# Moving weight preparation and eight up products of a feed-forward network into the start of a two-layer transformer kernel

## The chip, the cores and the metric

The kernel runs on one core of a Trainium2 chip. The core has five engines that work side by side, each on its own queue of instructions: TensorE (PE, matrix products and transposes; PEld are its weight loads), VectorE (DVE), ScalarE (ACT, activation functions), GpSimd (POOL) and SyncE (SP, which here only issues DMA transfers). The metric is device time in microseconds for one launch. The time before is 1350.04 us, the median of three runs (1349.27 to 1352.81).

## The reference

The input is 2 batches of 1024 tokens with 256 features, float32. Two layers are computed; in each, attention and a feed-forward network (FFN) read the same normalized input, and both are added to it:

```python
xn = _layernorm(x, axis=-1)
x = x + _L0_attn_ref(xn, Wq, Wk, Wv, Wp, bp) + _L0_ffn_ref(xn, W_fc, W_proj)
xn = _layernorm(x, axis=-1)
x = x + _L1_attn_ref(xn, ...) + _L1_ffn_ref(xn, w1, w2, w3)
```

What matters here is layer 0. Its attention has 16 heads of 16 features and is causal. Its FFN first turns its weights into ternary ones, in groups of 64, and then has an up product to 1024 hidden features, a squared relu, an RMS norm, and a down product:

```python
scale = clip(mean(abs(wg)), 1e-08, None)          # wg: groups of 64, in bfloat16
q = clip(round(wg / scale), -1.0, 1.0)
w1 = w + ((q * scale) - w)                        # so for W_fc and for W_proj
h = square(relu(einsum('bsd,hd->bsh', x, w1)))
hn = h * rsqrt(mean(square(h)) + eps)
out = einsum('bsh,dh->bsd', hn, w2)
```

Layer 1 has a latent attention, which makes up the second half of the kernel's time, and an FFN with a sigmoid gate (`sigmoid(x1) * x2`) whose weights are ternary too, with one scale for a whole matrix.

## The kernel before

All work is in float32 and the order on every engine is written out by hand: under `tc.manual_schedule()` each engine executes its instructions in the order in which the Python code emits them. An instruction waits on its own engine until its inputs are there and its output buffer is free, and everything behind it on that engine waits too.

**Tiles.** The tokens lie in 16 tiles of 128 (0 to 7 are batch 0). The rows of `x` are loaded in four transfers, even and odd tiles of each batch (`even`, `odd`, `even1`, `odd1`). `ln_stats` (VectorE statistics, then a square root on ScalarE, L157 to L161), `ln_rstd` (reciprocal on VectorE, L169), `ln_norm` (the normalized pair of tiles, on VectorE or GpSimd, L179, one buffer) and `ln_turn` (transpose on TensorE, L190; copied out by ScalarE, L196) make the transposed input `xnT`.

**Attention.** The heads of one batch are worked on in four groups of four, eight groups in all. For a group, `project` makes keys (1), queries (0) or values (2) on TensorE (L240), evacuates them on ScalarE or VectorE (L248, L250) and writes them to DRAM; `fetch` (L262) reads them back in another order into the buffers `stage`, of which keys and values share one; `permute` (L269 to L273) puts them in their last layout as `head`. Of a batch's four groups, the first two need the even tiles alone, the other two the odd ones. Then come the maxima of the scores for each query (`maxima`, TensorE L313, reduced by VectorE, L324 and L329), `finish` (the maxima are added to the queries as one more row, L338 and L339), and later `scores` (L354), their exponential on ScalarE (L361), a causal mask on GpSimd (L364), and `product` with the values (L379).

The main loop runs over g from -1 to 8 and, within a group, over twelve steps n. In a step of a group, TensorE makes a piece of the maxima of the next group (g + 1), a piece of this group's scores, and a product from two steps back. Round g = -1 has only the maxima of group 0, and the dictionary `first` says what else is done in its steps: projections of the groups 1 to 3, norms, permutes.

**Fill.** `fill` is a list of pieces, one of which is popped in each step of a group: twelve projections of the groups 4 to 7, then for each of four blocks of 512 tokens the FFN of layer 0 as eight `up` products (L436; relu, square and again square on ScalarE, L443 to L449, and an accumulation of squares on GpSimd, L446 and L450) and eight `down` products (L467). From group 6, step 3, on, the FFN of layer 1 for two blocks is added behind (`ffn1`: `up` L578 with a sigmoid on ScalarE, L585; `down` L593). Group 7 has no next group and pops two pieces in each step. What is left is done among the output projections of batch 1.

**Ternary weights.** `ternary(w)` gives four pieces for one half of a weight matrix row block: `begin` (absolute value and sign on ScalarE, L205 and L207), `scale` (a sum over groups on TensorE, L211, then two operations on VectorE), `choose` (VectorE), and `put` (one operation on VectorE, two on GpSimd, L226 to L228). There are eight such steps, `weight_steps`: four for the up weights `wfc`, then four for the down weights `wpr`. `deal` puts a list of pieces into half steps of the main loop, and `slot` runs what is due. Before, all eight were dealt from group 0, step 0, on, one in two steps:

```python
for k, pieces in enumerate(weight_steps):
    deal(0, 2 * k, 0, pieces)
```

Buffers that matter: two pairs of PSUM banks for scores and the maxima of group 0 (`ps_s`), three single banks for all else (`ps_m`), six temporary tiles (`temp`) for evacuated projections, junk outputs, relu and squares, one buffer each for `q_ab`, `q_sg`, `q_sc` and `xn`.

Of the kernel before, what the change touches and what calls it, by code (L numbers as in the profile page):

```python
# [46 lines left out]
def two_layers(ctx: ExitStack, tc: tile.TileContext, a: dict, out: bass.AP):  # L47
    nc = tc.nc
# [57 lines left out]
    with ExitStack() as scope:  # L106
# [4 lines left out]
        NG = 4 * B  # L111
# [39 lines left out]
        xnT = [main.tile([P, KC, S], F32, tag=f"xnT{b}", name=f"xnT0_{b}") for b in range(B)]  # L151
# [11 lines left out]
        def ln_stats(at):  # L163
            for n in range(*at.indices(NT)):
                ln_stat(n)
            ln_root(at)

        def ln_rstd(at):
            nc.vector.reciprocal(rstd[:, at], rstd[:, at])  # L169
# [4 lines left out]
        def ln_norm(n, step=1, engine=nc.vector):  # L174

            xn = l0t.tile([P, SC], F32, tag="xn", name="xn", bufs=1)
            for k in range(2):
                t = n + k * step
                engine.tensor_scalar(  # L179
                    xn[:, k * E : (k + 1) * E], x_sb[:, t, :], mv[:, t, 0:1], rstd[:, t : t + 1],  # L180
                    ALU.subtract, ALU.mult,
                )
            return xn

        def ln_turn(xnT, n, xn, step=1):

            pt = ps_bank()
            for k in range(2):
                for kc in range(KC):
                    nc.tensor.transpose(  # L190
                        pt[:, (2 * kc + k) * P : (2 * kc + k + 1) * P],
                        xn[:, k * E + kc * P : k * E + (kc + 1) * P], ident,
                    )
            at = n % TB
            to = xnT[n // TB].rearrange("p c (n t) -> p c n t", t=P)[:, :, at : at + step + 1 : step, :]
            nc.scalar.copy(to, pt.rearrange("p (c n t) -> p c n t", c=KC, n=2))  # L196
# [61 lines left out]
        def fetch(g, i):  # L258

            src = rows[g, i].rearrange("(j d) t -> d j t", d=D0)  # L260
            for c in range(4):
                nc.sync.dma_start(stage[i][32 * c : 32 * c + D0], src[:, :, GC * c : GC * (c + 1)])  # L262
# [473 lines left out]

        with tc.manual_schedule():

            even, odd, even1, odd1 = EVEN_ODD
            ln_stats(even)  # L740
            ln_rstd(even)
            for n in (0, 4):
                ln_turn(xnT, n, ln_norm(n, 2), 2)
            project(0, 1, nc.vector)
            fetch(0, 1)
            project(0, 0)
            fetch(0, 0)
            ln_stats(odd)
            project(0, 2, nc.vector)
            project(1, 1)  # L750
            ln_stats(even1)
            ln_stats(odd1)
            for at in (odd, even1, odd1):
                ln_rstd(at)
            project(1, 0)
            project(1, 2, nc.vector)
            for n in (1, 5):
                ln_turn(xnT, n, ln_norm(n, 2, nc.gpsimd), 2)
            permute(0, 1)
            permute(0, 0)  # L760

            first = {
                0: [lambda: turns.append(ln_norm(8, 2, nc.gpsimd))],
                1: [lambda: fetch(0, 2), lambda: project(2, 1)],
                2: [lambda: ln_turn(xnT, 8, turns.pop(), 2), lambda: project(2, 0),
                    lambda: turns.append(ln_norm(12, 2, nc.gpsimd))],
                3: [lambda: project(2, 2)],
                4: [lambda: permute(0, 2), lambda: fetch(1, 1), lambda: fetch(1, 0),
                    lambda: ln_turn(xnT, 12, turns.pop(), 2)],
                5: [lambda: project(3, 1), lambda: turns.append(ln_norm(9, 2, nc.gpsimd))],  # L770
                6: [lambda: project(3, 0)],
                7: [lambda: permute(1, 1), lambda: ln_turn(xnT, 9, turns.pop(), 2),
                    lambda: turns.append(ln_norm(13, 2, nc.gpsimd))],
                8: [lambda: permute(1, 0)],
                9: [lambda: project(3, 2), lambda: ln_turn(xnT, 13, turns.pop(), 2)],
            }
            turns = []

            slots = {}

            def deal(g, n, part, pieces):
                for k, f in enumerate(pieces):
                    at = 2 * (12 * g + n) + part + k
                    slots.setdefault((at // 24, at % 24 // 2, at % 2), []).append(f)
# [2 lines left out]
                for f in slots.pop((g, n, part), ()):  # L787
                    f()

            for k, pieces in enumerate(weight_steps):  # L790
                deal(0, 2 * k, 0, pieces)
            deal(2, 4, 0, ternary1("w1"))
            deal(3, 4, 0, ternary1("w2"))
# [9 lines left out]
            for g in range(-1, NG + 1):  # L803
                this, nxt = 0 <= g < NG, g + 1 < NG
                for n in range(12 if g < NG else 2):
                    k = 12 * g + n - 2
                    if g == NG - 2 and n == 3:
                        fill += ffn1(0) + ffn1(1)
                    if g == -1:
                        for f in [maxima(0, n, pair) for pair in ((0, 1), (2, 3))]:  # L810
                            f()
                    elif nxt:
                        for part, (a_, b_) in enumerate((((0, 1), (2, 3)), ((2, 3), (0, 1)))):
                            after = [maxima(g + 1, n, a_), scores(g, n, b_)]
                            for f in after:
                                f()
                            if k >= 0 and part == 0:
                                product(k // 12, k % 12)
                            if part == 0:
                                slot(g, n, 0)  # L820
                    else:
                        if this:
                            after = [scores(g, n, pair) for pair in ((2, 3), (0, 1))]
                            for f in after:
                                f()
                            fill.pop(0)()
                        product(k // 12, k % 12)
                        slot(g, n, 0)
                    if k >= 0 and k % 12 in (3, 11):
# [64 lines left out]
            for i in range(TB):  # L894
                f = project_out(B - 1, i)
                if rest is not None:
                    rest()
                rest = f
                if i % 2 == 0 and fill:
                    pump()  # L900
                    pump()
                else:
                    side.pop(0)()
                if i == 4:
                    ln_stats(four(2))
                if i == 5:
                    ln_rstd(four(2))
                    xnT1.append(main.tile([P, KC, S], F32, tag="xnT1", name="xnT1_1"))
                    xn = ln_norm(8)
                if i == 6:  # L910
                    ln_turn(xnT1, 8, xn)
                    xn = ln_norm(10)
                if i == 7:
                    ln_turn(xnT1, 10, xn)
# [1 line left out]
            ln_stats(four(3))  # L916
            ln_rstd(four(3))
            xn = ln_norm(12)
            side.pop(0)()
            pump()  # L920
            ln_turn(xnT1, 12, xn)
            xn = ln_norm(14)
# [406 lines left out]
```

## Time and profile before

| what | value |
|---|---|
| median of three runs | 1350.04 us |
| the profiled execution | 1347.1 us, its span 1345.4 us |
| PE busy | 1277.3 us (95%) |
| DVE busy | 751.9 us (56%) |
| ACT busy | 673.0 us (50%) |
| POOL busy | 480.6 us (36%) |
| granted TensorE clock, mean | 0.976 |
| first piece of the maxima (L313) | 36.47 us from the start |
| first scores of group 0 (L354) | 79.25 us |
| last up product of group 7 (L578) | 588.15 us |

The busy time of an engine is the time in which it had an instruction at work, and at a lower clock the same work is longer busy. TensorE is busy for most of the span; where it isn't, or where its clock is below 1, time can be gained. The page gives the span in 40 slices of 33.6 us.

### The profile page before, as it was taken

How to read it: one execution, taken by the hardware profiler on the slowest of the kernel's cores; microseconds unless marked ns; L12 is line 12 of the kernel's file. 1: busy time of each engine (PE TensorE's matmuls, PEld its weight loads, DVE VectorE, ACT ScalarE, POOL GpSimd, SP SyncE). 2: the span in 40 equal slices, each digit the busy share in tenths (PEclk: the TensorE clock that was granted, in tenths of full speed). 3: DMA queues.
4: the chain of work that ended last, by engine and by line, in shares of the span. 5: the costliest groups of instructions: out<-in, count | busy, mean ns of one | idle time of the engine just before them, and what ended most of it. 6: DMA issues, size and time to landing. Idle time of an engine off the chain costs nothing.

```text
span 1345.4 us, 36539 instructions
## 1 busy us (share of the span) xinstructions
PE 1277.3 (95%) x15722; PEld 794.5 (59%) x15722; DVE 751.9 (56%) x1879; ACT 673.0 (50%) x1250; POOL 480.6 (36%) x506
## 2 busy tenths in 40 slices
PE   5899999999999999999998799999999999999996
PEld 3454445464564643556757467777666767767665
DVE  3557755565465562124335676666656666666572
ACT  1235664646537556554233565555455555555541
POOL 4333733543224221010231444433444434444310
PEclk9779999999999998999998999999999999999998
DMA  7221301011010000001043000000000000000000
GB/s 230 55 56 55 95 1 25 1 25 16 10 16 9 25 1 20 17 1 59 1 145 74 14 18 11 14 22 11 22 15 22 7 26 10 27 10 15 15 6 22
DMA packets 65810, 41.11 MB, mean 31 GB/s; under 512 B 37841, under 2 KB 63185, under 8 KB 65393
## 3 DMA queue, kind: packets, MB, share of 16 engines
q1 hardware_dynamic: 64800, 35.51, 10.5%
q8 instruction: 123, 2.02, 0.6%
q0 software_dynamic: 416, 2.49, 0.5%
q10 hardware_dynamic: 432, 0.79, 0.2%
q14 instruction: 39, 0.31, 0.1%
HBM read 26.18 MB, written 10.49 MB: 27 GB/s over the span
## 4 chain that ended last, share of the span: by engine, by line
PE 82%; DVE 5%; ACT 3%; issue 3%; POOL 1%; DVEq 0%; ACTq 0%; POOLq 0%
PE ps_s L1090 15%; PE ps_m L313 12%; PE ps_o L1138 11%; PE ps_m L578 6%; PE ps_o L379 5%; PE ps_t L1030 5%; PE ps_m L467 5%; PE ps_m L436 5%; PE ps_m L593 3%; PE ps_t L1023 3%; PE ps_t L1165 3%; DVE p L1097 2%; PE ps_m L240 2%; DVE pT L1107 1%; ACT p L1101 1%
## 5 line engine op out<-in xcount | busy, mean ns | idle before, releaser
L1101 ACT ACTIVATE p<-p,nmax 128x1024 f32<-128x1024 f32 (+7 forms) x256 | 197.2, 771 | 210.7 <-DVE nmax L1097 209.8
L1090 PE MATMUL ps_s<-kT,qc 128*128 128x512 f32 (+3 forms) x768 | 280.9, 499 | 19.0 <-DVE nmax L1097 10.3
L1097 DVE CUSTOM_DVE_ANT_0 p<-ps_s,wpe 128x1024 f32<-128x1024 f32 (+7 forms) x256 | 184.9, 745 | 176.5 <-PE ps_s L1090 175.5
L361 ACT ACTIVATE p<-ps_s 128x1024 f32<-128x1024 f32 (+1 forms) x192 | 153.0, 809 | 138.0 <-PE ps_s L354 133.1
L1090 PEld LDWEIGHTS ps_s<-kT,qc 128*128 128x128 f32 x768 | 131.2, 191 | 130.8 <-issue 94.6
L1107 DVE STREAM_TRANSPOSE pT<-p 128x1024 f32<-128x1024 f32 (+7 forms) x256 | 185.9, 758 | 22.1 <-ACT p L1101 21.0
L313 PE MATMUL ps_m<-head,head 16*128 16x512 f32 (+3 forms) x672 | 180.4, 539 | 2.8 <-DVE nmx L324 1.2
L354 PE MATMUL ps_s<-head,head 17*128 17x512 f32 (+3 forms) x768 | 167.0, 539 | 0.0
L1138 PE MATMUL ps_o<-pT,vrep 32*64 32x128 f32 x9216 | 153.5, 276 | 7.3 <-issue 4.5
L1138 PEld LDWEIGHTS ps_o<-pT,vrep 32*64 32x64 f32 x9216 | 136.1, 132 | 35.8 <-issue 28.7
L1063 POOL TENSOR_TENSOR qc<-t,t 32x512 f32<-32x512 f32 x120 | 152.4, 1270 | 8.1
L364 POOL TENSOR_SCALAR_AFFINE_SELECT p<-p 128x256 f32<-128x256 f32 x128 | 55.1, 436 | 219.7 <-ACT p L361 219.3
L1058 POOL TENSOR_TENSOR t<-t,cosq 128x512 f32<-128x512 f32 x28 | 35.7, 1273 | 257.9 <-issue 143.9
L313 PEld LDWEIGHTS ps_m<-head,head 16*128 16x128 f32 x672 | 68.8, 185 | 91.6 <-issue 31.5
L578 PE MATMUL ps_m<-xnT,w 128*128 128x512 f32 x192 | 94.3, 619 | 0.0
L329 DVE TENSOR_REDUCE nmx<-ps_m 128x1 f32<-128x512 f32 x112 | 72.3, 686 | 38.0 <-PE ps_s L354 28.8
L324 DVE CUSTOM_DVE_ANT_0 junk<-ps_m,maskz,nmx 128x512 f32<-128x512 f32 (+3 forms) x112 | 57.7, 548 | 47.3 <-PE ps_s L354 33.0
L379 PE MATMUL ps_o<-p,v 128*32 128x512 f32 (+3 forms) x768 | 82.5, 502 | 0.0
L467 PEld LDWEIGHTS ps_m<-wpr,hT 128*128 128x128 f32 x512 | 59.9, 191 | 16.6 <-DVE nmx L324 6.0
L467 PE MATMUL ps_m<-wpr,hT 128*128 128x128 f32 x512 | 66.6, 282 | 0.0
L1165 PE MATMUL ps_t<-wvo,xT 128*128 128x256 f32 x256 | 62.3, 387 | 4.4 <-DVE nmax L1097 2.6
L324 DVE CUSTOM_DVE_ANT_0 junk<-ps_m,maskz 128x512 f32<-128x512 f32 (+3 forms) x112 | 50.6, 488 | 27.8 <-PE ps_s L354 22.6
(172 smaller groups left out, 1783.2 us busy)
## 6 DMA issues: line engine op xcount, KB each, us to landing
rows<-proj SPq DMA_DIRECT2D x24, 256.0 KB, 2.2
stage<-rows SPq DMA_DIRECT2D x96, 64.0 KB, 3.2
w<-in_w SPq DMA_DIRECT2D x3, 768.0 KB, 5.0
x_sb<-in_x SPq DMA_DIRECT2D x4, 512.0 KB, 12.2
x<-x_sb SPq DMA_DIRECT2D x4, 512.0 KB, 3.2
fold_wo<-in_wo SPq DMA_DIRECT2D x8, 256.0 KB, 3.1
vrep<-kv SPq DMA_DIRECT2D x32, 64.0 KB, 2.1
xin<-x SPq DMA_DIRECT2D x16, 128.0 KB, 2.2
```

The source lines that it names most:

```text
L313: nc.tensor.matmul(t[:, :w], quad(q, c, D0)[:, i * P : (i + 1) * P], quad(k, c, D0)[:, k0 : k0 + w], start=True, stop=True, tile_position= ...
L354: nc.tensor.matmul(t[:, c % 2, :w], quad(k, c, D0 + 1)[:, j * P : (j + 1) * P], quad(q, c, D0 + 1)[:, at : at + w], start=True, stop=True, ...
L361: nc.scalar.activation(p[:, pair[0] : pair[0] + 2, :w], t[:, :, :w], AF.Exp)
L379: nc.tensor.matmul(quad(box["o"], c)[:, SC - w :], values[g][:, j, 32 * c : 32 * c + 32], p[:, c, :w], start=(j == 0), stop=(j == 4 * iq + ...
L467: nc.tensor.matmul(po[:, :P], f["h", hc // 2][:, hc % 2, t * P : (t + 1) * P], wpr[:, hc, cols], start=(hc == 0), stop=(hc == NH0 - 1),)
L578: nc.tensor.matmul(pw, w1t[f"w{i + 1}"][:, kc, hc * P : (hc + 1) * P], xnT1[n // 2][:, kc, (n % 2) * SC : (n % 2 + 1) * SC], start=(kc == ...
L1063: (even, odd)[x].tensor_tensor(self.qc[64 + 32 * x : 96 + 32 * x, hh], t1[at : at + 32], t2[at : at + 32], ALU.add,)
L1090: nc.tensor.matmul(sc[:, j * SC + n0 : j * SC + n1], s.q[k].qc[:, h // QP, h % QP, :], kT[:, s.b * S + n0 : s.b * S + n1], start=True, sto ...
L1097: nc.vector.tensor_tensor_reduce(p, sc[:, j * SC : j * SC + w], maskw[:, S - w :], -1.0, 3.0e38, ALU.add, ALU.min, nmax,)
L1101: nc.scalar.activation(p, p, AF.Exp, bias=nmax, scale=-1.0, accum_out=s.rsum[:, k, h : h + 1])
L1107: nc.vector.transpose(s.pT[:, at, h, :], s.p[k, h])
L1138: nc.tensor.matmul(s.o[64 * hh : 64 * hh + 64, c, k * P : (k + 1) * P], vrep[32 * c : 32 * c + 32, s.b * 32 + sb, :], s.pT[32 * c : 32 * c ...
```

## The change

Three things are changed, all of them in the order of work; what is computed stays the same.

First, the statistics of the odd tiles move ahead of the first projection, and the first two of the eight ternary steps are made among the first projections. Steps three and four are dealt to the steps 0 to 6 of round g = -1, and the four steps of the down weights to group 0, steps 0 to 7. Second, eight pieces (the `up` products of the first block of layer 0's FFN) are taken out of `fill` and done in the steps 1, 2, 3, 4, 7, 8, 10 and 11 of round g = -1. Third, the first two permutes go in front of the turn of the tiles 5 and 7 and behind the turn of 1 and 3; the norms of the odd tiles are made on GpSimd between the ternary steps, and the statistics of batch 1 come later, behind the last projection and in step 0.

As `fill` is eight pieces shorter, layer 1's FFN is added from group 5, step 8, on, and group 7 pops a second piece only in every third step.

```diff
             even, odd, even1, odd1 = EVEN_ODD
+            first_w, second_w = weight_steps[0], weight_steps[1]
             ln_stats(even)
             ln_rstd(even)
             for n in (0, 4):
                 ln_turn(xnT, n, ln_norm(n, 2), 2)
+            ln_stats(odd)
+            ln_rstd(odd)
+            first_w[0]()
             project(0, 1, nc.vector)
             fetch(0, 1)
+            first_w[1]()
             project(0, 0)
             fetch(0, 0)
-            ln_stats(odd)
+            first_w[2]()
+            first_w[3]()
+            second_w[0]()
+            turns = [ln_norm(1, 2, nc.gpsimd)]
             project(0, 2, nc.vector)
+            second_w[1]()
             project(1, 1)
+            second_w[2]()
+            second_w[3]()
+            ln_turn(xnT, 1, turns.pop(), 2)
+            turns.append(ln_norm(5, 2, nc.gpsimd))
+            permute(0, 1)
+            project(1, 0)
+            permute(0, 0)
+            project(1, 2, nc.vector)
             ln_stats(even1)
-            ln_stats(odd1)
-            for at in (odd, even1, odd1):
-                ln_rstd(at)
-            project(1, 0)
-            project(1, 2, nc.vector)
-            for n in (1, 5):
-                ln_turn(xnT, n, ln_norm(n, 2, nc.gpsimd), 2)
-            permute(0, 1)
-            permute(0, 0)
-
+            ln_rstd(even1)
+
+            def odd_ones():
+                ln_stats(odd1)
+                ln_rstd(odd1)
+            up = lambda: fill_up.pop(0)()
+            fill_up = fill[12:20]
+            del fill[12:20]
             first = {
-                0: [lambda: turns.append(ln_norm(8, 2, nc.gpsimd))],
-                1: [lambda: fetch(0, 2), lambda: project(2, 1)],
-                2: [lambda: ln_turn(xnT, 8, turns.pop(), 2), lambda: project(2, 0),
+                0: [lambda: ln_turn(xnT, 5, turns.pop(), 2), odd_ones,
+                    lambda: turns.append(ln_norm(8, 2, nc.gpsimd))],
+                1: [lambda: fetch(0, 2), lambda: project(2, 1), up],
+                2: [lambda: ln_turn(xnT, 8, turns.pop(), 2), lambda: project(2, 0), up,
                     lambda: turns.append(ln_norm(12, 2, nc.gpsimd))],
-                3: [lambda: project(2, 2)],
+                3: [lambda: project(2, 2), up],
                 4: [lambda: permute(0, 2), lambda: fetch(1, 1), lambda: fetch(1, 0),
-                    lambda: ln_turn(xnT, 12, turns.pop(), 2)],
+                    lambda: ln_turn(xnT, 12, turns.pop(), 2), up],
                 5: [lambda: project(3, 1), lambda: turns.append(ln_norm(9, 2, nc.gpsimd))],
                 6: [lambda: project(3, 0)],
-                7: [lambda: permute(1, 1), lambda: ln_turn(xnT, 9, turns.pop(), 2),
+                7: [lambda: permute(1, 1), lambda: ln_turn(xnT, 9, turns.pop(), 2), up,
                     lambda: turns.append(ln_norm(13, 2, nc.gpsimd))],
-                8: [lambda: permute(1, 0)],
+                8: [lambda: permute(1, 0), up],
                 9: [lambda: project(3, 2), lambda: ln_turn(xnT, 13, turns.pop(), 2)],
+                10: [up],
+                11: [up],
             }
-            turns = []
...
-            for k, pieces in enumerate(weight_steps):
+            for k, pieces in enumerate(weight_steps[2:4]):
+                for x, f in enumerate(pieces):
+                    deal(-1, 3 * k + x, 1, [f])
+            for k, pieces in enumerate(weight_steps[4:]):
                 deal(0, 2 * k, 0, pieces)
...
-                    if g == NG - 2 and n == 3:
+                    if g == NG - 3 and n == 8:
                         fill += ffn1(0) + ffn1(1)
...
-                            fill.pop(0)()
+                            if n % 3 == 0:
+                                fill.pop(0)()
```

Two more edits guard the list `side` behind the groups against being empty.

More of the change, by code (lines that the diff above doesn't have):

```diff
@@ L901, in two_layers @@
                     pump()
-                else:
+                elif side:
                     side.pop(0)()
@@ L918, in two_layers @@
             xn = ln_norm(12)
-            side.pop(0)()
+            if side:
+                side.pop(0)()
             pump()
```

## The prediction

> **What bounds the kernel now.** I read, in this order: the page's slices, the windows by stage, the timeline of the first 80 us, and the chain of waits behind it.
>
> ```profile
> PE   5899999999999999999998799999999999999996
> ...
> PEclk9779999999999998999998999999999999999998
> ```
>
> Each digit is a tenth of one 33.6 us slice. TensorE is the bound nearly everywhere; the first two slices have room, and slices 2 and 3 run below full clock. So work taken out of TensorE's later queue is worth its full time if the start can take it up free. The windows (columns: stretch, length, then busy us of PE, PEld, DVE, ACT, POOL, the granted clock, DMA share, GB/s) show the start and, last, a later stage:
>
> ```profile
> 32.00:36.00 4.00, 1.38 (x4) 0.57 (x4) 0.00 (x0) 2.00 (x2) 3.09 (x4) 0.50 0.18 30
> 36.00:40.00 4.00, 2.09 (x8) 0.51 (x8) 1.30 (x5) 0.42 (x1) 0.56 (x1) 0.50 0.00 0
> ...
> 72.00:76.00 4.00, 4.00 (x16) 2.94 (x14) 0.68 (x4) 0.60 (x1) 0.00 (x0) 0.50 0.00 0
> ...
> 80.00:84.00 4.00, 4.00 (x13) 1.80 (x12) 2.57 (x8) 3.09 (x4) 2.38 (x3) 0.50 0.00 0
> 84.00:88.00 4.00, 4.00 (x16) 2.36 (x16) 0.97 (x2) 0.60 (x1) 0.37 (x1) 0.66 0.00 0
> 88.00:92.00 4.00, 4.00 (x18) 2.54 (x15) 3.50 (x11) 1.62 (x2) 1.68 (x3) 0.77 0.86 167
> 92.00:96.00 4.00, 4.00 (x31) 1.87 (x31) 1.40 (x6) 2.23 (x4) 2.54 (x3) 0.81 0.63 97
> ...
> 140.00:200.00 60.00, 59.79 (x399) 26.91 (x398) 37.69 (x100) 40.56 (x60) 32.59 (x34) 1.00 0.20 49
> ```
>
> TensorE idles until 36.5 us, and "4.00 busy" at clock 0.50 is half the work. The timeline says why it idles:
>
> ```profile
> 25.01 1.78 SPq L262 DMA_DIRECT2D stage<-rows  x4
> ...
> 34.00 0.59 ACT L196 COPY xnT<-ps_m 128x512 f32<-128x512 f32 x1 [2.76 <-PE ps_m L190]
> ...
> 34.49 1.93 ACT L271 COPY head<-stage 128x1024 f32<-128x1024 f32 x1
> 36.47 0.51 PEld L313 LDWEIGHTS ps_s<-head,head 16*128 16x128 f32 x8 [2.90 <-ACT head L271]
> ```
>
> The last query fetch is issued at 26.3 and lands 3.1 us later, at 29.4; its permute on ScalarE starts 5.1 us after that, because it stands behind the evacuation of a transpose (L196) whose norm POOL made. From there the chain is TensorE's own work:
>
> ```profile
> 82.78 3.71 PE ps_m L240 x8
> ...
> 95.89 1.94 PE ps_m L240 x8
> ...
> 147.11 1.92 PE ps_m L436 x4
> ```
>
> A projection (L240) costs 1.94 us at full clock, 3.71 at half; an up product of layer 0's FFN (L436) 1.92, on the chain.
>
> [...] 0.50 from about 29 to 46 us, after TensorE had run dry at 26.6; but it also falls to 0.50 at 72 to 76 with TensorE called busy[...]. [...] the trace has one norm half on POOL at 2.06 us where the others take 1.22.
>
> **The change, part by part.**
>
> *Moved out of TensorE's later time.* Eight up products, 8 x 1.92 = 15.3 us, leave the groups; in effect the last group pops 16 pieces instead of 24, since everything queued shifts forward by eight. With them go the four scale matmuls of the up weights (L211, four of its pieces on the chain: 0.39 + 0.21 + 0.22 + 0.22 = 1.0). Sum 16.3 us less after group 0 begins. TensorE is 59.8 of 60 us busy in those stages, so nothing else hides it. In the last group one sigmoid per two pieces costs ScalarE 0.60 and two table loads, 3.2 us. Over its steps 3 to 11 I count 33 us for ScalarE (exps 13.6, six sigmoids 19, a copy) against 38 for TensorE (12 ups 23, scores 8, products 7): TensorE stays the bound; price 0, at worst 6 us where the two collide. One more table load in all, 1.3 us on ScalarE: hidden.
>
> *Before the first maxima.* The second norm statistics (DVE, 2.2 us) go ahead of the first projection's evacuation. Their input landed at 11.4 us and VectorE is free from 12.0 to 17.3: cost 0. The up weights landed at 2.3 + 8.8 = 11 us, so the ternary's Abs and Sign (2 x 0.62 on ScalarE) start at 14.5 and wait for nothing. VectorE's share per step is 0.69 + 0.43 + 0.69 + 0.94 = 2.75; two steps lie in its gaps and end at 24.7, just after the key fetch landed (21.6 + 3.0 = 24.6), so the key permute (1.02) runs at about 25 rather than 27.4. POOL: first put 20.6 to 23.2 (2 x 1.27), norm 1 to 25.6, second put to 28.2, norm 5 to 30.6. TensorE waits for norm 1 (projections end at 23.4, transpose ends 26.3), then makes the last two projections of group 1. SP issues the same writes and fetches in the same order, and its fetch at 25.01 waits only for the issues before it. ScalarE's query permute now stands behind one evacuation, not two transposes: 29.4 to 31.4, and the maxima start at 31.4 instead of 36.5. If the pause to 26.3 halves the clock, those two projections take 3.7 us each and the start is 34.6. I take 32.5.
>
> *The first maxima, longer.* TensorE's list at full clock: twelve maxima 11.1 (rows of 1.14, 0.93, 0.71, 0.50 by width), six projections 11.5, five transposes of norms 3.3, finish and values 1.5, eight ups 15.4, two scale matmuls 0.4: 43.2 us. Today it is 26.8, and takes 42.3 (36.5 to 78.8): VectorE's reductions (24 us) feed it, gaps open, the clock falls. With an up of 1.9 us in most steps VectorE gets ahead, except at the start: the statistics of the second batch (2 x 2.2 us) now stand between the first reductions, and I find 2.5 us of waits in steps 0 to 2. ScalarE gains relu, square, square (0.60 + 0.63 + 0.63) per up, 15 us, and Abs and Sign 2.5: about 28 of 45 us. POOL gains an accumulate per up (1.27, 10 in all) and two puts (5.1) beside norms 9.7 and permutes 5.9: 31 of 45 us. It is strict in order: norm 12 stands behind two accumulates (ready 51.7, wanted 51.4: 0.3 us lost), up 4 needs the last put (63.8 against 63.0: 0.8). The value permute ends at 57.5 rather than 52.0, behind a put; SP's two fetches queued behind it land at 62.3 and 64.2; the key permute of group 1 then holds ScalarE to 64.4 with an evacuation behind it, and POOL's query permute ends at 73. Both are in time for group 0. Squared tiles wait in the six temporary buffers for POOL; I find no wait over half a microsecond.
>
> *Clock.* Half rate at the beginning of this stage: 0 to 9 us; denser work speaks for little, today's start for much. I take 3. Group 0 then starts at 32.5 + 43.2 + 2.5 + 1.1 + 3 = 82.3, against 78.8: 3.5 lost. Today group 0 itself loses 4 x (0.50 + 0.34 + 0.23 + 0.19) = 5.0 us to the clock (the four windows from 80). This may go entirely or not; I take half, 2.5 gained.
>
> *Sum.* 16.3 - 3.5 + 2.5 = 15.3 us. The profiled execution took 1347.1 (span 1345.4), so 1332; the runs' median is 1350.04, 3 above it, and on that scale 1335. Bounds: start at 31.4, no half rate anywhere, gain 22 (1328); start at 34.6, 9 us of half rate, group 0 as slow as now: 16.3 - 11.6 = 5 (1345).
>
> **Rivals.** (1) *The clock stays halved as it is today.* The maxima are thin matmuls that use 16 of the array's rows each, and the clock sank at 72 while TensorE was busy. Maxima to 88.3, group 0 unchanged: gain 7, 1343. For: the windows above. Against: ups are full-array work. (2) *The last group becomes ScalarE's.* With one up per step TensorE's step is 4.0 us and ScalarE's with a sigmoid 5.1; if each of six collides (about 2 us each, 12), gain 3, 1347. Against: the step without sigmoid takes ScalarE only 1.9, and two score buffers even it out. (3) *POOL's order becomes the bound, slower.* Accumulates wait for ScalarE's squares, and norms 12, 9, 13, the last put and the permutes wait behind them; norms have one buffer. If each of these five places stalls TensorE by 4 us and the clock falls after each (another 6), group 0 starts at 104: 25 later, loss 9, 1359. It decides once group 0 starts after 95 (78.8 + 16.3). For: only 0.3 us of slack at norm 12 and none at the last put, by my own count. Against: POOL is busy 31 of 45 us, so what is late in one step is caught up in the next.
>
> **How the numbers follow.** Forecast 0.64 (its own range 1328 to 1342), rival 1 0.17, rival 2 0.09, rival 3 0.10. About 0.3% (4 us) is what this kernel's measurement tells from no change. Faster: the forecast and nearly all of rival 1, 0.79; same: rival 2 and a remainder, 0.11; slower: 0.10. Range 1326 to 1348: it takes in rivals 1 and 2 and the bounds, and leaves out rival 3 and a tail below.
>
> **What would show it.** The first L313 near 32 us (not 36); group 0's first L354 at 78 to 86; eight L436 groups of 1.9 us between them; clock digits of slices 2 and 3 above 7; the last L578 of the last group and everything after it about 15 us earlier. I am wrong if L190 or L436 wait long on POOL, if the clock stays at 0.5 to 60 us, or if scores (L354) in the last group wait for ScalarE.

## The result and the profile after

The changed kernel takes 1335.12 us, the median of four runs (1331.33 to 1338.34), against 1349.65 of four runs of the kernel before (1347.56 to 1352.81): a ratio of 0.989, with a 95% interval of 0.985 to 0.993. The profiled execution took 1332.75 us, its span 1331.1 us, at a mean granted clock of 0.991; before it was 1347.1, 1345.4 and 0.976. The forecast was 1335 for the median and 1332 for the profiled execution.

The two rows of the page that answer to those of before, the busy tenths of TensorE and its granted clock in 40 slices:

```profile
PE   5999999999999999998997899999999999999996
...
PEclk9899999999999999999999999999999999999999
```

The second slice is fuller (9 instead of 8), and slices 2 and 3 of the clock row are at 8 and 9 where they were at 7 and 7. The stretches of 4 us behind these digits, in the columns of the same table of before (start:end, length, busy us of PE, PEld, DVE, ACT, POOL, the clock, DMA share, GB/s):

```profile
36.00:40.00 4.00, 4.00 (x12) 1.93 (x11) 3.50 (x16) 1.04 (x3) 0.99 (x1) 0.50 0.02 6
40.00:44.00 4.00, 4.00 (x11) 2.36 (x9) 1.44 (x7) 0.90 (x2) 0.00 (x0) 0.71 0.05 19
...
72.00:76.00 4.00, 4.00 (x19) 2.15 (x18) 3.42 (x13) 2.54 (x5) 3.71 (x4) 1.00 0.00 0
80.00:84.00 4.00, 4.00 (x26) 1.91 (x25) 1.25 (x10) 3.23 (x6) 1.27 (x1) 1.00 0.22 50
84.00:88.00 4.00, 4.00 (x21) 1.96 (x16) 2.61 (x8) 3.94 (x6) 2.87 (x2) 1.00 0.00 0
...
92.00:96.00 4.00, 4.00 (x31) 2.36 (x33) 3.02 (x11) 1.92 (x4) 2.96 (x4) 1.00 0.80 128
```

The beginning of the first maxima still runs at half rate (0.50 and 0.71 in the two windows from 36 us). From 44 us to the end of group 0 the clock is at 1.00 but for one dip (0.85 and 0.73 in the two windows from 60 us), and group 0 (83.0 to 112.0 us) has no half rate at all (1.00). The timeline around the start (start, length, engine, line, output and inputs, and in brackets the idle time before and what ended it):

```profile
29.63 1.95 ACT L271 COPY head<-stage 128x1024 f32<-128x1024 f32 x1
...
31.64 1.14 PE L313 MATMUL ps_s<-head,head 16*128 16x512 f32 x8 [0.81 <-ACT head L271]
...
34.25 0.69 DVE L324 CUSTOM_DVE_ANT_0 junk<-ps_s,maskz 128x512 f32<-128x512 f32 x1
...
35.62 2.88 PE L313 MATMUL ps_s<-head,head 16*128 16x384 f32 x8 [2.25 <-DVE nmx L324]
```

The query permute starts 0.5 us after its last fetch has landed (issued at 26.2, landed 2.9 us later, at 29.1), and the maxima start 4.8 us earlier than before. Then TensorE waits 2.25 us for the first reduction, because VectorE makes statistics of batch 1 first (from 31.55 us on, ahead of the reduction at 34.25).

The time by stages, worked out from the starts of lines and the span (us; the last column is after minus before):

| stage | before | after | difference |
|---|---|---|---|
| to the first maxima (L313) | 36.5 | 31.6 | -4.8 |
| first maxima, to group 0's first scores (L354) | 42.8 | 51.3 | +8.6 |
| to the first finished output of a group (L386) | 32.1 | 29.1 | -3.0 |
| to the last finished output of group 7 (L386) | 479.6 | 464.9 | -14.7 |
| the rest | 754.5 | 754.2 | -0.3 |

The second row has a large spread of its own: another execution of the kernel before took 49.0 us there (experiment 5). The gain is made in the groups, as intended. But the fourth row is the sum of three things; one of them the prediction priced at nothing, and one it did not have. The last group, over its own stretch (the same columns), before:

```profile
537.20:590.90 53.70, 53.65 (x328) 25.28 (x328) 9.00 (x20) 34.74 (x41) 6.19 (x14) 1.00 0.03 11
```

and after:

```profile
526.40:576.90 50.50, 49.05 (x252) 17.36 (x250) 6.66 (x13) 34.74 (x41) 6.58 (x15) 0.97 0.03 11
```

It has 328 - 252 = 76 fewer matmul records, but is only 3.2 us shorter, and ScalarE is busy for the same 34.74 us. The chain of waits says who sets the end. Before, in this group, shares by line:

```profile
by line: PE ps_m L578 42.5%; PE ps_m L593 22.7%; PE ps_o L379 17.2%; PE ps_s L354 15.5%; PE ps_m L393 1.6%; ACT oT L386 1.1%; PE ps_m L338 0.2%; issue 0.0%
```

After, with one stretch of its pieces (start, length, what):

```profile
by line: PE ps_m L578 24.3%; PE ps_s L354 15.6%; ACT p L361 14.5%; ACT L361 10.5%; issue 10.4%; PE ps_o L379 9.8%; PE ps_m L593 4.8%; ACT L585 3.8%; ACT sg L585 2.4%; PE ps_m L393 1.7%; POOL p L364 1.5%; ACT oT L386 1.2%; PE ps_m L338 0.9%
...
557.89 0.70 ACT L585
558.60 0.59 issue
559.19 0.60 ACT sg L585
...
559.80 1.28 ACT L361
...
561.10 1.03 ACT p L361
...
562.17 1.83 PE ps_s L354 x8
```

Before, the chain is TensorE's but for 1%. After, ScalarE's lines and the "issue" between them (parts of its table loads) are 14.5 + 10.5 + 10.4 + 3.8 + 2.4 = 42% of it: a table is loaded for the sigmoid (1.28), the sigmoid runs (0.60), the table of the exponential is loaded back (1.28), and only then the exponential releases the next scores. That is rival 2 of the prediction, in part, and the last of its own signs of being wrong: scores in the last group wait for ScalarE. What the last group loses, something else must have given back; the experiments size the loss and find where the rest came from.

### The profile page after: what moved, and what is told of

Read it like the earlier page. It is cut to its first block, busy times and chain, and to the rows that moved or that the text cites. A ratio compares the mean times of both kernels' runs of the same rounds, so it can differ in the third digit from the quotient of the medians.

```text
span 1331.1 us, 36533 instructions
## 1 busy us (share of the span) xinstructions
PE 1261.8 (95%) x15722; PEld 787.8 (59%) x15722; DVE 749.8 (56%) x1879; ACT 674.7 (51%) x1251; POOL 479.3 (36%) x506
## 3 DMA queue, kind: packets, MB, share of 16 engines
q1 hardware_dynamic: 64800, 35.51, 10.5%
## 4 chain that ended last, share of the span: by engine, by line
PE 83%; DVE 6%; ACT 5%; issue 3%; POOL 2%; DMA 0%; DVEq 0%; ACTq 0%; POOLq 0%
PE ps_s L1115 15%; PE ps_m L313 12%; PE ps_o L1163 11%; PE ps_o L379 5%; PE ps_m L578 5%; PE ps_t L1055 5%; PE ps_m L467 5%; PE ps_m L436 4%; PE ps_m L593 3%; PE ps_m L240 3%; PE ps_t L1048 3%; PE ps_t L1190 3%; DVE p L1122 2%; DVE pT L1132 1%; ACT p L1126 1%
## 5 line engine op out<-in xcount | busy, mean ns | idle before, releaser
L1132 DVE STREAM_TRANSPOSE pT<-p 128x1024 f32<-128x1024 f32 (+7 forms) x256 | 185.9, 758 | 22.4 <-ACT p L1126 21.3
L313 PE MATMUL ps_m<-head,head 16*128 16x512 f32 (+3 forms) x672 | 178.3, 533 | 3.4 <-DVE nmx L324 1.3
L354 PE MATMUL ps_s<-head,head 17*128 17x512 f32 (+3 forms) x768 | 167.7, 533 | 1.1 <-ACT p L361 1.1
L1083 POOL TENSOR_TENSOR t<-t,cosq 128x512 f32<-128x512 f32 x28 | 35.7, 1273 | 258.7 <-issue 144.0
L313 PEld LDWEIGHTS ps_m<-head,head 16*128 16x128 f32 x672 | 67.2, 183 | 88.1 <-issue 29.3
```

Source lines behind the costliest of these rows:

```text
L313: nc.tensor.matmul(t[:, :w], quad(q, c, D0)[:, i * P : (i + 1) * P], quad(k, c, D0)[:, k0 : k0 + w], start=True, stop=True, tile_position= ...
L354: nc.tensor.matmul(t[:, c % 2, :w], quad(k, c, D0 + 1)[:, j * P : (j + 1) * P], quad(q, c, D0 + 1)[:, at : at + w], start=True, stop=True, ...
L1132: nc.vector.transpose(s.pT[:, at, h, :], s.p[k, h])
```

## The experiments

The main theory at the outset, A, is that of the prediction: the gain is the moved work, above all the eight up products; the weights alone bring little, and the permutes in front buy the early start. Against it stands that the ups are largely given back in the last group, and that the gain comes from the weights, the norms' order and the clock. Each expectation says what it weighs. All ratios are against the kernel before on the same chip (1349.51, 1349.39 and 1349.69 us in three batches).

**1. No early up products.** The pieces stay in `fill`; group 7 pops two in each step, as before.

```diff
-            fill_up = fill[12:20]
-            del fill[12:20]
+            fill_up = [lambda: None] * 8
...
-                    if g == NG - 3 and n == 8:
+                    if g == NG - 2 and n == 3:
...
-                            if n % 3 == 0:
-                                fill.pop(0)()
+                            fill.pop(0)()
```

> The changed kernel, but the eight up products stay in the fill list and group 7 pops two pieces in every step, as before. Theory A (TensorE is the bound from group 0 on, and what pays is its work taken out of the groups, less what the first maxima grow): the maxima start at 31.6 us as in the changed kernel, take about the 42 us they took before, group 0 starts near 74, and most of the gain is lost: 1343 to 1346, with the last group as long as before. Theory B (the gain is the clock, which dense up products hold up): clock of the maxima as low as before, 0.976 in the mean, and no gain, 1348 to 1351. Theory C (the gain is the earlier start of the maxima): as the changed kernel, 1335 to 1338.

Measured: 1339.02 us, 0.992 (0.991 to 0.994). The up products are worth 1339.0 - 1335.1 = 3.9 us of the 14.5, not most of it. The stages of its profile say why. With the ups, the round of the first maxima goes from 45.7 to 51.3 us, group 0's beginning from 32.1 to 29.1, and the stretch from the first to the last finished output from 473.2 to 464.9. The last, 8.3 us less, is about half of the ups' 15.3. Experiment 9 finds the other half.

**2. Permutes late.** The permutes go behind the turn of the tiles 5 and 7, as before; all else is as changed.

```diff
-            permute(0, 1)
             project(1, 0)
-            permute(0, 0)
             project(1, 2, nc.vector)
+            ln_turn(xnT, 5, turns.pop(), 2)
+            permute(0, 1)
+            permute(0, 0)
...
-                0: [lambda: ln_turn(xnT, 5, turns.pop(), 2), odd_ones,
+                0: [odd_ones,
```

> The changed kernel, but the first two permutes stand behind the turn of tiles 5 and 7 again, and that turn ahead of the maxima. Theory A: the start of the maxima goes from 31.6 to about 36; part of it is won back, since the statistics of batch 1 then no longer stand between first maxima and their reductions: 3 to 5 us lost, 1338 to 1341. Theory C: the whole gain is lost, 1346 to 1350. Theory B: no loss so long as the ups are there, 1334 to 1337.

Measured: 1334.03 us, 0.988 (0.986 to 0.991): nothing lost. The first maxima start at 34.5 instead of 31.6, but their round takes 50.0 instead of 51.3 us, and group 0 starts at 84.5 instead of 83.0; by the end of group 7 the two are level (576.6 and 576.9). The permutes in front are worth nothing that these runs can measure. (Its last group takes 48.9 us instead of 50.5, without the half rate that the changed kernel has there from 544 to 552 us.)

**3. Statistics early.** The 2.25 us wait on VectorE is removed: the statistics of batch 1 are made ahead of the last two projections.

```diff
             permute(0, 1)
+            for at in (even1, odd1):
+                for n in range(*at.indices(NT)):
+                    ln_stat(n)
             project(1, 0)
             permute(0, 0)
             project(1, 2, nc.vector)
-            ln_stats(even1)
+            ln_root(even1)
+            ln_root(odd1)
             ln_rstd(even1)
+            ln_rstd(odd1)
             def odd_ones():
-                ln_stats(odd1)
-                ln_rstd(odd1)
+                pass
```

> The changed kernel, but VectorE's statistics of batch 1 are made before the last two projections of group 1, where VectorE waits from 25.8 to 30.9 us, and the square roots and reciprocals behind the query permute. The changed kernel's trace has TensorE waiting 2.25 us for the first reductions and then half the clock from 36 to 42. If that wait is what lets the clock fall, 2 us of wait and about 3 us of half rate go, 1330 to 1333. If the clock falls for thin work anyway, 2 us or less, 1333 to 1335. If the round is bound later by POOL or VectorE, no gain, 1335.

Measured: 1333.97 us, 0.989 (0.987 to 0.991), the same as the changed kernel. The maxima start at 33.4 and group 0 at 82.5, against 31.6 and 83.0: the wait behind the first maxima is gone (TensorE idles 0.9 us there instead of 2.25), but the last two projections run at a clock of 0.57 (28 to 32 us, 1.00 in the changed kernel), and the maxima start 1.7 us later.

**4. Weights and norms alone.** The edits of 1 and 2 together: neither early ups nor early permutes.

> Neither early up products nor early permutes: of the change only the order of the weight steps, norms and statistics is left. Theory A: four scale matmuls, 1 us, and lighter VectorE queues in group 0, against longer queues at the start: 1347 to 1351. If the weights' early preparation by itself delays the first maxima (rows of ternary work on VectorE and GpSimd ahead of the odd norms), slower than 1351. Theory B: as before, 1350.

Measured: 1338.48 us (1337.16 to 1347.56), 0.993 (0.991 to 0.996). 11.0 us of gain remain where A has 1347 to 1351: in that form A has fallen. From here to experiment 2, which adds the ups, it is 4.4 us, as from experiment 1 to the change: the ups are worth about 4 in both pairs.

**5. The kernel before once more**, one execution, for its clock.

> The kernel before, once more, for a second trace. In the first trace TensorE's clock fell to half at 412 to 420 and at 508 to 520 us, inside groups whose order of instructions is the same in the two runs with the weights moved alone, and there it did not. If these falls belong to the kernel before, they are seen again at the same places, within 10 us. If they are chance, they are gone or elsewhere, and the mean clock stays between 0.972 and 0.980 only because others take their place.

Measured: 1351.59 us, within the range of the kernel's other runs. The falls of the clock come back at the same work; they are taken up below. But the start differs: the first maxima start at 35.2 us and group 0 at 84.1, so that their round takes 49.0 us at a mean clock of 0.67, against 42.8 at 0.77 in the first profile. The 6.2 us between two executions of one kernel are half rate (49.0 x 0.33 = 16 us lost to it, against 42.8 x 0.23 = 10). So one profile of each kernel doesn't show a difference of that size in this round. What holds over all fourteen profiles is the clock: the six kernels with the up products in the round have a mean of 0.90 to 0.93 there, the eight executions without them 0.67 to 0.80. Whether it is the dense work of the ups, as the prediction guessed, or the gaps that they fill, no run tells apart.

**6 and 7. The gate without its table.** To show that the last group is short because of the sigmoid's tables, the gate of layer 1's FFN in the fill blocks is made as 1 / (1 + exp(-x)), the exponential on ScalarE, sum and reciprocal on VectorE; in the changed kernel (6) and in the kernel before (7).

```diff
-                    nc.scalar.activation(f["sg"], pw, AF.Sigmoid)
+                    if n < 2:
+                        nc.scalar.activation(f["sg"], pw, AF.Exp, scale=-1.0)
+                        nc.vector.tensor_scalar(f["sg"], f["sg"], 1.0, None, ALU.add)
+                        nc.vector.reciprocal(f["sg"], f["sg"])
+                    else:
+                        nc.scalar.activation(f["sg"], pw, AF.Sigmoid)
```

> The changed kernel, with the gate of layer 1's FFN for batch 0 made as 1 / (1 + exp(-x)): an exponential on ScalarE, and a sum and a reciprocal on VectorE, so that ScalarE needs no table load between gate and scores. Theory D (with fewer fill pieces the last group is bound by ScalarE, whose chain showed exps and table loads in the changed kernel: worth some 5 us): the second half of the last group goes from 31.6 us to about 27 and the time to 1328 to 1331. If TensorE is the bound there, as the prediction had it: no gain, 1334 to 1336. If VectorE's two more operations are long: slower, over 1337.

> The kernel before with the same gate by exponential. Theory D: its last group pops two pieces in every step and is TensorE's, so table loads are hidden: no gain, 1347 to 1350. If table loads cost time in both alike: as much faster as the changed kernel gets.

Measured: 1361.33 us, 1.009 (1.007 to 1.012), and 1369.94 us, 1.016 (1.014 to 1.018): both slower, for a reason that the first expectation names but gives no price. The group of the reciprocals in the profile of 6 (line, engine, operation, count | busy us, mean ns of one | idle before):

```profile
L588 DVE RECIPROCAL sg<-sg 128x512 f32<-128x512 f32 x12 | 40.2, 3353 | 0.4
```

3.35 us each, on an engine that has the maxima of the next group to reduce: group 6 is held up by it, and ends at 557.5 us instead of the changed kernel's 526.4. The last group has no next group, and there the pair of runs does answer. Its two halves (between the three outputs L386 from the end of group 6 to the end of group 7) take 16.0 and 27.9 us in 6, against 18.9 and 31.6 in the changed kernel; in 7, its second half takes 36.6 us, exactly as in the kernel before. So the sigmoids cost the last group several us after the change, and nothing in that half before it.

**8. The weights inside the first maxima.** The kernel before with its own beginning; the four steps of the up weights are dealt to round -1, those of the down weights from group 0, step 2, on.

```diff
-            for k, pieces in enumerate(weight_steps):
-                deal(0, 2 * k, 0, pieces)
+            for k, pieces in enumerate(weight_steps[:4]):
+                for x, f in enumerate(pieces):
+                    deal(-1, 3 * k + x, 1, [f])
+            for k, pieces in enumerate(weight_steps[4:]):
+                deal(0, 2 * k + 2, 0, pieces)
```

> The kernel before with its own start (odd norms, statistics and permutes as they were), but all four steps of the up weights in the steps of the first maxima and the four of the down weights from group 0, step 2, on. The run with weights, norms and statistics moved but neither ups nor permutes was 11 us faster than before, which theory A (1 us) doesn't explain. If taking VectorE and ScalarE work out of groups 0 and 1 is what pays: 1338 to 1342. If the reordered start (maxima 2.3 us earlier, odd norms at once) pays: 1346 to 1349. If neither, but the clock in later groups: anything, with the clock in proportion (0.983 for 1339, 0.976 for 1348).

Measured: 1354.96 us, 1.004 (1.002 to 1.005): 5.6 us slower. The round of the first maxima as a window, in the first profile of the kernel before and then here:

```profile
36.47:79.25 42.78, 38.85 (x175) 21.80 (x177) 25.00 (x78) 9.99 (x14) 11.19 (x9) 0.77 0.23 56
```

```profile
35.70:85.99 50.29, 44.18 (x180) 23.55 (x181) 34.19 (x92) 14.21 (x22) 19.45 (x15) 0.70 0.20 48
```

VectorE does 9.2 us more in a round in which TensorE waits for its reductions, 5.4 us here and 3.8 before. The round is 7.5 us longer than in that profile, at a clock of 0.70, but only 1.3 longer than in the other one (49.0 at 0.67). That VectorE's longer list makes this version slower is likely by these waits, but not shown. Of the changed kernel:

```profile
31.64:82.97 51.33, 48.29 (x212) 25.93 (x212) 35.68 (x107) 23.96 (x40) 27.30 (x22) 0.90 0.25 57
```

It gives VectorE as much (35.7 us), but has TensorE's own work to lay beside it, and the mean clock is 0.90.

**9. The gate in the last group alone.** As 6, but for the second of the two blocks alone (`if n == 1`); its six gates among the fill all fall in group 7.

> The changed kernel with the gate by exponential for block 1 alone, whose up products all lie in the last group, where VectorE was busy 2 to 3 of 20 us; its reciprocal takes 3.35 us. In the run with both blocks so, the two halves of the last group took 16.0 and 27.9 us, against 18.9 and 31.6 in the changed kernel, while group 6 lost 30. Theory D (ScalarE's table loads bind the last group of the changed kernel): both halves as in that run, 6 us less, 1328 to 1331. If the shorter halves only made up for work pushed ahead: 1334 to 1336. If VectorE's reciprocals hold the last down products: over 1336.

Measured: 1327.25 us (1323.61 to 1331.58), 0.984 (0.982 to 0.985). This is the best version: 7.9 us below the changed kernel and 22.4 below the kernel before. Its last group, as a window and by the chain of waits from 526 to 577 us (L598 is the L593 of before, five lines further down):

```profile
528.80:572.70 43.90, 43.84 (x252) 16.15 (x250) 28.20 (x24) 19.21 (x29) 6.60 (x15) 1.00 0.04 13
```

```profile
by line: PE ps_m L578 45.0%; PE ps_o L379 18.9%; PE ps_s L354 18.1%; PE ps_m L598 12.6%; PE ps_m L393 3.0%; ACT oT L386 1.2%; PE ps_m L338 0.9%; PE ps_m L406 0.6%; issue 0.1%
```

The same 252 matmuls take 43.9 us instead of 50.5, ScalarE falls from 34.7 to 19.2 us (the twelve table loads of 1.28 us), VectorE takes 28.2 without harm, and the chain is TensorE's again. The changed kernel's last group loses 50.5 - 43.9 = 6.6 us to ScalarE, 1.7 of them as half-rate time (0.93 and 0.64 in the two windows from 544 us, 4 x (0.07 + 0.36)) that follows a wait of 0.85 us for an exponential. Little of it shows as idle time of TensorE, which is called busy for 49.05 of the 50.50 us: the eight score matmuls of a step with 512 columns take 1.14 us together here, and up to 2.04 in the changed kernel, where the second half of them waits for an exponential.

**10. The order alone.** The norms, statistics and so on in the order of experiment 4, with all eight ternary steps where they were before. Against experiment 4:

```diff
-            first_w[0]()
...
-            second_w[3]()
...
-            for k, pieces in enumerate(weight_steps[2:4]):
-                for x, f in enumerate(pieces):
-                    deal(-1, 3 * k + x, 1, [f])
-            for k, pieces in enumerate(weight_steps[4:]):
+            for k, pieces in enumerate(weight_steps):
                 deal(0, 2 * k, 0, pieces)
```

> No weight step, up or permute moved: of the change only the order of norms and statistics at the start (odd statistics ahead of the first projection, the odd norms on GpSimd at once, statistics of batch 1 late). Weights are made from group 0 on as before. Theory E (the two weight steps in VectorE's and ScalarE's idle time before the first maxima are what pays in the run with weights moved alone): no gain, 1347 to 1351. Theory F (the order of norms is what pays, since the maxima start 2 us earlier and their clock rises sooner): 1339 to 1345. Part of both: 1343 to 1347.

**11. Two weight steps alone.** The order of before, with the pieces of two ternary steps put between its projections.

```diff
             for n in (0, 4):
                 ln_turn(xnT, n, ln_norm(n, 2), 2)
+            first_w, second_w = weight_steps[0], weight_steps[1]
+            first_w[0]()
             project(0, 1, nc.vector)
...
             project(1, 1)
+            second_w[2]()
+            second_w[3]()
...
-            for k, pieces in enumerate(weight_steps):
+            for k, pieces in enumerate(weight_steps[2:]):
```

> The kernel before, its norms and statistics in their old order, with the first two weight steps among the first projections; the other six from group 0, step 0, on, one in two steps. Theory E: most of the gain of the weights alone, 1340 to 1344. Theory F: no gain or a loss, 1348 to 1353, since the odd norms on GpSimd come later by the two puts (5.1 us of GpSimd work ahead of them).

Measured: order alone 1344.99 us, 0.996 (0.995 to 0.998), 4.7 us of gain; two weight steps alone 1348.07, 1.000 (0.999 to 1.001), none. In experiment 4 order and weights (four steps early instead of two) give 11. The profile of 10 looks like no gain, with a span only 1.0 us shorter than in the first profile of before; but its round of the first maxima (48.0 us at 0.68) is like that of the second. Against that one its span is 5.5 us shorter, 3.3 of it at the start (31.9 instead of 35.2). What the order saves the weights from is in the timeline of 11:

```profile
30.43 3.29 POOL L179 TENSOR_SCALAR xn<-x_sb,ln_mv,ln_rstd 128x256 f32<-128x256 f32 x2 [1.80 <-issue]
...
32.57 0.44 PE L190 MATMUL ps_m<-ident,xn 128*128 128x128 f32 x2 [4.98 <-POOL xn L179]
...
40.32 1.24 PE L313 MATMUL ps_s<-head,head 16*128 16x512 f32 x4 [2.50 <-ACT head L271]
```

The norm of the odd tiles stands on GpSimd behind both puts, TensorE waits 4.98 us for it, and the maxima start 3.9 us later than before. In the changed order the norm goes between the puts.

**12. The best version with late permutes**, 9 and 2 together.

> Late permutes (no slower than the changed kernel in its run) together with the gate by exponential for block 1: 1 us less than the changed kernel with that gate at best, equal to it within the noise at worst, 1327 to 1331. If the gate brings nothing: 1333 to 1336.

Measured: 1328.58 us, 0.985 (0.983 to 0.987). It cannot be told from 9, and agrees with 2: where the permutes stand doesn't matter.

**The clock in the later groups.** What balanced the loss of the last group shows in the kernel before, far from the places that the change touches. Its windows in groups 5 and 6:

```profile
412.00:416.00 4.00, 3.69 (x25) 1.75 (x26) 0.96 (x8) 2.17 (x5) 2.52 (x3) 0.80 0.00 0
416.00:420.00 4.00, 4.00 (x26) 1.26 (x24) 1.29 (x2) 2.57 (x4) 2.15 (x4) 0.77 0.29 66
...
508.00:512.00 4.00, 3.28 (x20) 0.74 (x22) 1.25 (x4) 2.56 (x4) 0.00 (x0) 0.75 0.00 0
512.00:516.00 4.00, 4.00 (x11) 1.46 (x12) 1.16 (x4) 1.02 (x2) 1.51 (x3) 0.50 0.00 0
516.00:520.00 4.00, 4.00 (x28) 1.27 (x27) 2.16 (x8) 1.16 (x2) 0.41 (x1) 0.90 0.01 2
```

These cost 4 x (0.20 + 0.23) = 1.7 and 4 x (0.25 + 0.50 + 0.10) = 3.4 us. They come back at the same work in the second execution of the kernel before (4 to 5 us later) and in experiment 10 (order alone), and the second of them in 8. The profiles of 1, 2, 3, 4, 9, 11 and 12 have no window below 0.97 from 116 to 576 us, the changed kernel only those of its last group. So the spells are absent wherever the first two weight steps stand ahead of the first maxima, and one or both are there where they don't (6 and 7, whose reciprocals hold up these groups, are left out). How a step made there could reach so far, none of the runs shows. The work around the first spell, before:

```profile
412.31 0.37 PE L313 MATMUL ps_m<-head,head 16*128 16x128 f32 x1 [0.71 <-ACT relu L443]
...
413.95 3.38 PE L436 MATMUL ps_m<-xnT,wfc 128*128 128x512 f32 x4
```

and the same work in experiment 4:

```profile
407.92 0.37 PE L313 MATMUL ps_m<-head,head 16*128 16x128 f32 x1 [0.71 <-ACT relu L443]
...
409.56 1.98 PE L436 MATMUL ps_m<-xnT,wfc 128*128 128x512 f32 x4
```

The same wait of 0.71 us stands before an up product of 3.38 us in one and of 1.98 us in the other, and for 103 us ahead of the wait some 700 matmuls of TensorE follow one another at the same distances in both traces, to 0.02 us. So neither this wait nor those 103 us of work decide it. What does, no run here shows, and the cause stays open.

## Why the prediction was right, and where it was not

**The bound and the start.** Right. The first L313 came at 31.6 us (32.5 taken, bounds 31.4 and 34.6), group 0 at 83.0 (82.3 taken), 3.7 later than before. The prediction has 3.5 for this, but counts from 78.8 us, where the table ahead of it has 79.25; against the table its forecast was 3.1. The 2.5 us of waits in the first steps are there, 2.25 of it at one place. Of the two waits on GpSimd that I had counted, 0.3 us at norm 12 is 0.36 at 54.8 us; the 0.8 before an up product is 0.2, at a weight load. That the pause before the last two projections could halve the clock was an estimate; TensorE waits 1.59 and 1.46 us there, the clock is 1.00 from 24 to 32 us, and the two take 3.62 us together. The early permutes were part of this chain of reasoning, and there it was right about the start and wrong to count the start as time: experiment 2 starts 2.9 us later and loses nothing.

**The clock at group 0.** 2.5 us taken, half of 5.0; group 0's beginning is 3.0 shorter. That the two are near is chance: the half rate went entirely, not by half, but TensorE now idles 0.9 us there, which accounts for a part of the 2.0 that are lost again. Rival 1 is out: the round's mean clock is 0.90 instead of 0.77 or 0.67, and group 0 is at 1.00. Rival 3 is out: group 0 starts 12 us ahead of the 95 at which it would decide. Experiment 8 is a slower version; the waits of its round are for VectorE's reductions, none for GpSimd.

**The last group: the step that failed.** "TensorE stays the bound; price 0, at worst 6 us where the two collide." It lost 6.6 us, as experiment 9 measures, and 5.0 in the profile of experiment 2 (48.9 against 43.9), where the clock doesn't fall in this group. I had set ScalarE's 33 us against TensorE's 38 over nine steps, as sums, and took the larger; but scores, exponential and product follow one another with two score buffers, and two table loads of 1.28 us fall between an exponential and the next. Rival 2 had the mechanism and put its price too high (12 us).

**The term that was missing.** The half-rate spells of 5.1 us in the groups 5 and 6 of the kernel before. I had shown the windows to 96 us and a later stage at clock 1.00, and took all later stages to be like it. The clock row of before, which the prediction quotes, has an 8 as its 16th digit (504 to 538 us), where the larger spell lies; I didn't follow it. The fourth row of the stages is then -16.3 for the moved work, -5.1 for the spells and +6.6 for ScalarE: -14.8, against -14.7 measured. The size of the moved work itself was right: from experiment 1 to experiment 9, neither of which has the spells or a last group that waits for ScalarE, this stretch goes from 473.2 to 458.2 us, 14.9 less for the ups' 15.3. The forecast of the time was right by luck, because a loss that I priced at nothing and a gain that I had not seen lie within 1.5 us of each other.

**Whose gain it is.** The prediction put 15.3 of the 16.3 us that leave the groups on the ups, and 3.5 against them for the longer start. The runs put some 4 us net on the ups in the changed kernel, 11 on the order of the norms together with the early weights (4.7 on the order alone) and nothing on the permutes. The ups are worth so little mainly because the last group has become ScalarE's: from experiment 1 to experiment 9, where it is TensorE's again, the median falls by 11.8 us. (That the other gate by itself saves nothing there is in experiment 7, with 36.6 us in the second half as before.)

From experiment 10 to 4, which adds the weights, the median falls by 6.5 us. The profiles show 6.4 less in the later groups: 5.1 for the absent spells, the rest close to the 1.0 of the four scale matmuls. So most of what the weights gain hangs on spells whose cause isn't known. The profiles also have a round of the first maxima that is 5.8 us shorter, after a start 2.4 later, but two executions of the kernel before differ as much in this round.

## What to carry to other kernels

Work that is moved out of a stage is worth its time only for as long as the engine that it leaves is still the bound there: walk the other engine's chain, table loads (1.28 us each here) included, at the new density, instead of comparing sums. Preparation put into idle time of helper engines has to stand behind what TensorE waits for next: two weight steps in front of the odd norms gained nothing, four inside the first maxima lost 5.6 us, and with the norms between them the early weights came with a gain of 6.5. A total that agrees doesn't prove its parts: look through every stage of the kernel before for lowered clock, take a second profile before explaining a difference of one stage, and test the parts apart.

## What was not expected of the hardware

- A reciprocal of 128x512 float32 on VectorE takes 3.35 us (experiments 6 and 9), where an evacuation of the same shape (L250) takes 0.69.
- A table load takes 1.28 us each time in the changed kernel's last group, and where its input is ready, the next activation starts within 0.02 us of its end (559.80 + 1.28 = 561.08, and 561.10): a change of table for one sigmoid and back costs 2 x 1.28 us.
- TensorE can be called busy for all of a stretch at half rate (4.00 of 4 us at a clock of 0.50, 512 to 516 us of before and 36 to 40 of after), and the same work with the same wait of 0.71 us in front runs halved in one kernel and not in another (an up product of 3.38 us before, 1.98 in experiment 4).
